# Attention's running states: summed by TensorE in PSUM and copied by ScalarE, in place of additions on VectorE

## The chip, the core and the metric

The kernel runs on one core of one Trainium2 chip, in one launch. A core has five engines with an instruction stream each: TensorE (PE in the profile; its weight loads are shown apart as PEld), VectorE (DVE), ScalarE (ACT), GpSimd (POOL) and SyncE (SP, which here only issues DMAs). They meet through semaphores. TensorE writes its results to PSUM, a memory in banks, from which VectorE and ScalarE read.

The metric is the device time of one execution, in microseconds, as the median of several runs.

## The reference

A group normalization and causal linear attention are added to x, then a group normalization and a chain of four Mamba blocks. The change touches the attention, whose core is this (x is 8 x 512 x 48 x 48, so 8 samples of L = 2304 positions with 8 heads of 64):

```python
def _feature(t):
    return jax.nn.elu(t) + 1.0
...
def step(S, qkv):
    q, k, v = qkv
    S = S + k[..., :, None] * v[..., None, :]
    o = jnp.einsum('nhk,nhkv->nhv', q, S)
    return (S, o)
_, outs = jax.lax.scan(step, S0, (Qs, Ks, Vs))
...
den = 1.0 / (jnp.einsum('nhld,nhld->nhl', Q, jnp.cumsum(K, axis=1)) + 1e-10)
num = _linear_causal_numerator(Q, K, V)
out = num * den[..., None]
...
x = x + _L0_conv_ref(_gn(x), L0_conv_Wq, L0_conv_bq, L0_conv_Wkv, L0_conv_bkv)
x = x + _L1_conv_ref(_gn(x), L1_conv_in_proj_w, ...)
```

For each head there is a running state S of 64 x 64, the sum of k v^T over all earlier positions. The kernel needs it only at the borders of blocks of 128 positions: within a block it uses the masked product of q and k.

## The kernel before

**The work.** Attention is cut into 8 samples x 4 pairs of heads x 6 chunks of 384 positions, 192 calls of the generator `chunk`. A chunk has NT = 3 blocks of T = 128 positions. Mamba is cut in the same way into 192 jobs (two streams of samples, taking turns); a job has 8 slots. A slot is four scans on VectorE (`scan`, L894, each over a decay that ScalarE writes to a PSUM bank, `decay`, L883), one product ahead of them (L873 on VectorE, L862 on GpSimd), one weighing by C on GpSimd (`weigh`, L906) and eight products on TensorE that gather the result (`gather`, L922). Before a job come its convolution (L698), gate (L709), SiLU, the small products for dt, B and C (L745, L758), and the softplus (L769).

**What sets the order.** The program writes out the order by hand. `slot` emits four scans, and between them calls `beside` twice, so that there are 16 half slots to a job. `chunk`, `prepare` and the other generators yield a due time in half slots and the number of PSUM banks they need next; `beside` steps those that are due and whose banks are free. So one chunk runs along with one job, always at the same place in it. Each engine executes its instructions in the order in which they were emitted.

**The banks.** Six PSUM banks (`spare`) are handed out to whoever takes one: chunks, job preparation and decays. ScalarE is up to three decays ahead of the scans (`DEPTH`, `ahead`); a bank that a scan or a chunk sets free is taken by a later decay.

**The state in a chunk.** `S` holds four states of 64 columns for both heads of the pair (128 partitions), one pair of heads over its six chunks. A chunk starts from the last state of the chunk before and makes the next three (`more`, two in the last chunk); `place` lists their columns, upward in even chunks and downward in odd ones, so that the last state of one chunk is the first of the next. Around the change:

- step `at(12)` takes a bank `both`. TensorE writes the denominators to its first six columns (L408) and the three sums k v^T of single blocks to columns 192 to 383 (`ds`, L413: for each block and each head one product of 64 x 64).
- step `at(14)`: VectorE reads the denominators (L416), takes the reciprocal (L417), and makes each state from the one before: a copy for the very first (L423), and otherwise an addition of `ds` to the state (L425). Each addition needs the last one's result. Then the bank is free.
- `at(15)`: ScalarE spreads the reciprocals over 64 columns (L429), TensorE turns them (L433), VectorE scales q (L438).
- `at(22)`: TensorE adds up x, S times q (L477) and v times the masked product (L486). The loop `while read[0] < m` at step `at(14)` holds the new states back until these products of the chunk before have been emitted.

All of these are float32. A float32 product appears as two TensorE records in the profile.

Of the kernel before, what the change touches and what calls it, by code (L numbers as in the profile page):

```python
# [17 lines left out]
P = 128  # L18
# [32 lines left out]
def attention_then_mamba_kernel(  # L51
# [12 lines left out]
    nc = tc.nc  # L64
# [17 lines left out]
    ident = cst[:, C_ID : C_ID + P]  # L82
# [200 lines left out]
    def chunk(m):  # L283


        b, o, c = parts[m]
        n = f"{b}_{o}_{c}"
        bank = Banks()
        NT = LC // T
        cols, tile_rows = slice(c * LC, (c + 1) * LC), slice(o * P, (o + 1) * P)  # L290
        subs = [slice(i * T, (i + 1) * T) for i in range(NT)]
        heads_of = [slice(par * 64, par * 64 + 64) for par in range(2)]

        def at(j, gap=1):
            return times[m] + j, gap

        def new(tag, bufs=1, shape=(P, LC)):
            return apool.tile(list(shape), F32, tag=tag, name=f"{tag}_{n}", bufs=bufs)
# [50 lines left out]
        S, stats, ksum = passes[b, o]  # L349
# [49 lines left out]
        kl, v = new("kl", 1, (P, NT, P)), new("v", 2, (P, NT, P))  # L399
# [8 lines left out]
            nc.tensor.matmul(den[:, 2 * i : 2 * i + 2], pr[:, subs[i]], hsel, start=True, stop=True)  # L408
        more = NT if c + 1 < NC else NT - 1
        ds = both[:, LC - NT * 64 : LC].rearrange("p (i d) -> p i d", i=NT)  # L410
        for i in range(more):
            for h in heads_of:
                nc.tensor.matmul(ds[h, i, :], kl[:, i, h], v[:, i, h], start=True, stop=True)  # L413
        yield at(14), 0
        rd = small.tile([P, 2 * NT], F32, tag="rd", name=f"rd_{n}", bufs=1)
        nc.vector.tensor_scalar_add(rd, den, 1e-10)  # L416
        nc.vector.reciprocal(rd, rd)  # L417
        while read[0] < m:
            yield "1w", 0
        place = range(NT + 1) if c % 2 == 0 else range(NT, -1, -1)  # L420
        for i in range(more):
            if c == 0 and i == 0:
                nc.vector.tensor_copy(S[:, place[1], :], ds[:, 0, :])  # L423
            else:
                nc.vector.tensor_add(S[:, place[i + 1], :], S[:, place[i], :], ds[:, i, :])  # L425
        bank.free()
        yield at(15), 0
        rdb = new("rdb", 1, (P, 2 * NT, 64))
# [15 lines left out]
        for sc in scs:  # L444
# [4 lines left out]
                start=True,  # L449
                stop=False,  # L450
                skip_group_check=True,
            )
        for i in range(NT):
            for h, sc in zip(heads_of, scs):
# [4 lines left out]
                    start=False,  # L459
                    stop=i == NT - 1,  # L460
                    skip_group_check=True,
# [11 lines left out]
        for i in range(NT):  # L473
            old = c > 0 or i > 0
            for h, sm in zip(heads_of, sms):
                if old:
# [4 lines left out]
                        start=False,  # L481
                        stop=False,
                        skip_group_check=True,
                    )
            for h, sm in zip(heads_of, sms):
# [4 lines left out]
                    start=False,  # L490
                    stop=i == NT - 1,
                    skip_group_check=True,
# [548 lines left out]
    def begin(latest):  # L1041

        nonlocal begun, put
        while counted and begins[counted[0]] - 4 <= half_no[0]:
            tasks.append(Task(statistics(counted.pop(0))))
        while put < len(parts) and times[put] - 6 <= half_no[0]:
            put += 1
            heads.append(Task(chunk(put - 1), before=heads[-1] if heads else None))
        while (
            begun < len(jobs)  # L1050
            and jobs[begun].start <= latest
            and jobs[begun].stream.block == jobs[begun].block
            and jobs[begun].stream.ready > jobs[begun].c
        ):
            tasks.append(Task(jobs[begun].prepare(), jobs[begun].start))
            begun += 1
# [241 lines left out]
```

## Time and profile before

| what | value |
|---|---|
| runs, median of 3 | 8507.66 us (8495.87 to 8511.29) |
| profiled execution, its own time | 8495.18 us |
| profiled execution, span from first to last instruction | 8493.4 us |
| TensorE's mean granted clock | 0.971 |
| scans on VectorE (L894) | 6144, busy 5448.0 us |
| state additions on VectorE (L425) | 512, busy 106.3 us |
| weighing on GpSimd (L906) | 1536, busy 4896.6 us |
| decays on ScalarE (L883) | 6144, busy 3422.1 us |
| gathering products on TensorE (L922) | 12288, busy 2374.3 us |

Busy times are of single engines and run beside each other, so they don't add up to the span. In lines of the profile `S<-S,bank` reads "writes S, reads S and a PSUM bank"; `L425` is a line of the kernel; `<-ACT bank L883` behind an idle time names what ended it, here a ScalarE instruction of line 883 that wrote a bank. Matmuls are pipelined: one record's length is its latency, and the distance between the starts of two records is what one costs in a row of them.

### The profile page before, as it was taken

The page shows a single profiled execution, that of the slowest core. Times are in us where ns is not written, and L with a number is a line of the kernel's source. Part 1 is how long each engine was busy: PE and PEld are TensorE (multiplying, and loading weights), DVE is VectorE, ACT ScalarE, POOL GpSimd, SP SyncE. Part 2 cuts the span into 40 slices and gives each one's busy share as a digit, 9 for nine tenths or more (in the row PEclk, how much of TensorE's full clock was granted, in tenths as well). Part 3 has the DMA queues.
Part 4 walks back from the last instruction along what each step waited for, and adds up shares of the span by engine and source line. Part 5 has one row for each costly group of instructions (what it writes and reads, how often), then busy time and mean ns, then how long its engine had stood idle before and what let it go on. Part 6 is the DMA issues. An engine that isn't in the chain of part 4 may idle for free. (4 is left out here: it accounts for less than half of the span.)

```text
span 8493.4 us, 124303 instructions
## 1 busy us (share of the span) xinstructions
PE 7728.9 (91%) x36482; PEld 3694.1 (43%) x36482; DVE 8077.7 (95%) x11078; ACT 6892.2 (81%) x14437; POOL 7761.5 (91%) x4235
## 2 busy tenths in 40 slices
PE   8799999999999999999999999999999999999965
PEld 4344444444444444444444444444444444444422
DVE  3799999999999999999999999999999999999998
ACT  3678888888888888888888888888888888888875
POOL 2689999999999999999999999999999999999998
PEclk9899999999999999999999999999999999999987
DMA  6567777767777777767777777777777777767655
GB/s 195 138 182 193 203 204 199 206 189 211 205 197 196 198 204 207 201 191 200 203 207 196 194 197 204 205 202 194 197 207 206 196 198 193 191 197 194 182 159 149
DMA packets 974426, 1654.38 MB, mean 195 GB/s; under 512 B 119337, under 2 KB 768169, under 8 KB 973618
## 3 DMA queue, kind: packets, MB, share of 16 engines
q1 hardware_dynamic: 973746, 1646.43, 70.6%
q8 instruction: 290, 4.75, 0.3%
q14 instruction: 390, 3.19, 0.1%
HBM read 1318.28 MB, written 327.68 MB: 194 GB/s over the span
## 5 line engine op out<-in xcount | busy, mean ns | idle before, releaser
L894 DVE TENSOR_TENSOR_SCAN u<-bank,u 128x385 f32<-128x385 f32 (+1 forms) x6144 | 5448.0, 937 | 138.5 <-ACT bank L883 136.6
L906 POOL TENSOR_TENSOR u<-u,C 128x1536 f32<-128x1536 f32 x1536 | 4896.6, 3188 | 498.3 <-DVE u L894 145.7
L883 ACT ACTIVATE bank<-dr,scales 128x385 f32<-128x385 f32 (+1 forms) x6144 | 3422.1, 578 | 788.1 <-DVE u L894 672.7
L922 PE MATMUL yp<-u,cst 128*64 128x384 f32 x12288 | 2374.3, 507 | 245.9 <-POOL u L906 126.8
L862 POOL TENSOR_TENSOR u<-B,dxr 128x512 f32<-128x512 f32 x1536 | 1973.4, 1285 | 47.7 <-DMA B<-scr 47.2
L873 DVE TENSOR_TENSOR u<-B,dxp 128x1024 f32<-128x1024 f32 x1536 | 1832.0, 1193 | 29.7 <-DMA B<-scr 24.2
L303 PE MATMUL bank<-xn,wq 128*128 128x384 f32 x4608 | 1741.1, 523 | 74.9 <-DVE u L894 39.6
L922 PEld LDWEIGHTS yp<-u,cst 128*64 128x64 f32 x12288 | 777.3, 138 | 1440.2 <-issue 926.3
L303 PEld LDWEIGHTS bank<-xn,wq 128*128 128x128 f32 x4608 | 869.1, 199 | 848.4 <-DVE u L894 139.9
L698 PE MATMUL bank<-xi,wk 128*128 128x384 f32 x3072 | 1107.4, 503 | 28.5 <-POOL xi L672 24.4
L698 PEld LDWEIGHTS bank<-xi,wk 128*128 128x128 f32 x3072 | 557.7, 191 | 575.9 <-issue 88.0
L315 ACT ACTIVATE ex<-bank,bqkv_sb 128x384 f32<-128x384 f32 x384 | 221.3, 576 | 470.7 <-PE bank L303 470.5
L883 ACT ACT_TABLE_LOAD x381 | 488.8, 1283 | 6.7
L811 POOL TENSOR_TENSOR dx<-delta,xs 128x384 f32<-128x384 f32 x384 | 387.3, 1009 | 33.0 <-ACT delta L769 33.0
L940 PE MATMUL bank<-yz,scales 128*128 128x384 f32 x768 | 305.0, 515 | 31.8 <-DVE yz L934 19.3
L433 PE MATMUL bank<-cst,rdb 128*128 128x128 f32 x576 | 102.9, 289 | 247.6 <-DVE u L894 244.1
L758 PE MATMUL bank<-dbc,steps_w 9*128 9x384 f32 x768 | 304.0, 515 | 3.1 <-ACT dbc L750 3.1
L709 PE MATMUL bank<-xi,scales 128*128 128x384 f32 x768 | 291.2, 493 | 10.6 <-ACT xs L734 8.8
L846 ACT COPY dxp<-dxr 128x512 f32<-128x512 f32 x384 | 226.7, 590 | 74.5 <-DMA dxr<-xscr 50.8
L745 PE MATMUL bank<-xs,scales 128*40 128x384 f32 x768 | 279.9, 486 | 0.3 <-ACT sm L467 0.3
L486 PE MATMUL bank<-sm,v 128*64 128x128 f32 x2304 | 253.4, 298 | 0.0
L734 ACT ACT_TABLE_LOAD x192 | 246.3, 1283 | 3.9 <-PE bank L698 0.6
(117 smaller groups left out, 7872.7 us busy)
## 6 DMA issues: line engine op xcount, KB each, us to landing
B<-scr SPq DMA_DIRECT2D x1536, 192.0 KB, 4.5
C<-scr SPq DMA_DIRECT2D x1536, 192.0 KB, 5.2
xn<-xn SPq DMA_DIRECT2D x192, 768.0 KB, 7.1
dr<-dscr SPq DMA_DIRECT2D x768, 192.0 KB, 3.8
dxr<-xscr SPq DMA_DIRECT2D x768, 192.0 KB, 4.9
dscr<-delta SPq DMA_DIRECT2D x192, 384.0 KB, 7.0
xscr<-dx SPq DMA_DIRECT2D x192, 384.0 KB, 2.4
xn<-in_x SPq DMA_DIRECT2D x48, 768.0 KB, 6.5
```

The source lines that it names most:

```text
L303: nc.tensor.matmul(ps, wqs[m // NC][:, kt, j * P : (j + 1) * P], xn[:, kt, :], start=(kt == 0), stop=(kt == 3),)
L698: nc.tensor.matmul(xc, wk[:, k, h * P : (h + 1) * P], xi[:, c0 + k : c0 + k + LC], start=(k == 0), stop=(k == 3),)
L709: nc.tensor.matmul(zp, w_gate[:, s, h * P : (h + 1) * P], xi[:, c0 + 3 : c0 + 3 + LC], start=True, stop=True,)
L758: nc.tensor.matmul(vp, steps_w[32:41, s, h * P : (h + 1) * P], dbc[32:41, :], start=True, stop=True)
L811: nc.gpsimd.tensor_tensor(dx[:, h, :], delta[:, h, :], xs[:, h, :], ALU.mult)
L862: nc.gpsimd.tensor_tensor(u[:, :, :, 1 + LC - TAIL :], self.B[s % 4][:, :, cols].unsqueeze(2).to_broadcast(shape), self.dxr[s // 4][:, :, ...
L873: nc.vector.tensor_mul(u[:, :, :, 1 : 1 + LC - TAIL], self.B[s % 4][:, :, cols].unsqueeze(2).to_broadcast(shape), self.dxp.unsqueeze(1).to ...
L883: nc.scalar.activation(dA[:, cols], self.dr[h][:, g, cols], AF.Exp, scale=w_a[:, self.w[1], 2 * h + g, q + j : q + j + 1],)
L894: nc.vector.tensor_tensor_scan(u[:, j, g, cols], dA[:, cols], u[:, j, g, cols], 0.0, ALU.mult, ALU.add,)
L906: nc.gpsimd.tensor_tensor(u[:, :, :, 0:LC], u[:, :, :, 1:], self.C[s % 4].unsqueeze(2).to_broadcast([P, NG, 2, LC]), ALU.mult,)
L922: nc.tensor.matmul(self.yp[g * 64 : g * 64 + 64, 0:LC], pair_sum, u[:, j, g, 0:LC], start=False, stop=(s % 4 == 3 and j == NG - 1), skip_g ...
L940: nc.tensor.matmul(self.xm[:, 0:LC], w_out[:, self.w[1], h, :], self.yz[:, h, :], start=(h == 0), stop=(h == 1),)
```

## The change

TensorE makes the running states itself, in the same columns of the same bank. An identity product first lays the old state `S[place[0]]` under all three new ones (from the second chunk on). Then the state after block i gets the products k v^T of all blocks 0 to i, added up in PSUM, in place of that of block i alone: twelve 64 x 64 products in place of six, or six in place of four in a last chunk. ScalarE copies all new states to `S` in one instruction, and the additions on VectorE go. `ds` is laid out in the order of the columns in `S`, so that the copy is one contiguous piece, also in odd chunks.

```diff
         more = NT if c + 1 < NC else NT - 1
         ds = both[:, LC - NT * 64 : LC].rearrange("p (i d) -> p i d", i=NT)
+        place = range(NT + 1) if c % 2 == 0 else range(NT, -1, -1)
+        low = min(place[1 : more + 1])
+        kept_states = slice(low, low + more)
+        if c:
+            nc.tensor.matmul(
+                ds[:, 0:more, :],
+                ident,
+                S[:, place[0], :].unsqueeze(1).to_broadcast([P, more, 64]),
+                start=True,
+                stop=False,
+                skip_group_check=True,
+            )
         for i in range(more):
-            for h in heads_of:
-                nc.tensor.matmul(ds[h, i, :], kl[:, i, h], v[:, i, h], start=True, stop=True)
+            for j in range(i + 1):
+                for h in heads_of:
+                    nc.tensor.matmul(
+                        ds[h, place[i + 1] - low, :],
+                        kl[:, j, h],
+                        v[:, j, h],
+                        start=c == 0 and j == 0,
+                        stop=j == i,
+                        skip_group_check=True,
+                    )
         yield at(14), 0
         rd = small.tile([P, 2 * NT], F32, tag="rd", name=f"rd_{n}", bufs=1)
         nc.vector.tensor_scalar_add(rd, den, 1e-10)
         nc.vector.reciprocal(rd, rd)
         while read[0] < m:
             yield "1w", 0
-        place = range(NT + 1) if c % 2 == 0 else range(NT, -1, -1)
-        for i in range(more):
-            if c == 0 and i == 0:
-                nc.vector.tensor_copy(S[:, place[1], :], ds[:, 0, :])
-            else:
-                nc.vector.tensor_add(S[:, place[i + 1], :], S[:, place[i], :], ds[:, i, :])
+        nc.scalar.copy(S[:, kept_states, :], ds[:, 0:more, :])
         bank.free()
         yield at(15), 0
```

## The prediction

> **What bounds the kernel now.** I read the page's busy shares, then the busy time by stretches, to see whether the start differs from the middle, then the groups of the lines that the change touches, then the timeline around one chunk of attention, and last the chain of waits through the same place.
>
> ```profile
> PE 7728.9 (91%) x36482; PEld 3694.1 (43%) x36482; DVE 8077.7 (95%) x11078; ACT 6892.2 (81%) x14437; POOL 7761.5 (91%) x4235
> ```
> ```profile
> 2000.00:3000.00 1000.00, 932.02 (x4462) 444.99 (x4462) 976.50 (x1328) 843.75 (x1778) 947.97 (x519) 0.99 0.73 199
> ...
> 0.00:340.00 340.00, 264.27 (x1325) 146.96 (x1327) 159.59 (x310) 151.06 (x305) 129.16 (x115) 0.92 0.59 176
> ```
>
> The second fence gives for two stretches their length and the busy us of PE, weight load, VectorE, ScalarE and GpSimd, then TensorE's clock, the DMA's share and GB/s. In the steady middle VectorE is busy 976 of 1000 us, the most of all; in the first 340 us it is busy 160 of 340, and nothing is gained there by relieving it.
>
> ```profile
> L425 DVE TENSOR_TENSOR S<-S,bank x512: 177/220/222, 46.5 to 8022.2; 128x64 f32<-128x64 f32 x171
> L423 DVE COPY S<-bank x32: 180/182/184, 46.3 to 7809.1; 128x64 f32<-128x64 f32 x32
> ...
>   ACT bank L883: 77.3, 143
> ```
>
> These are the state updates, 544 of some 0.2 us (shortest, median, longest in ns). ScalarE's next decay (L883) waited for the last of them 143 times, 0.54 us on average: it takes the PSUM bank that they set free.
>
> ```profile
> 7085.68 2.66 DVE L894 TENSOR_TENSOR_SCAN u<-bank,u 128x385 f32<-128x385 f32 x3 [0.79 <-ACT bank L883]
> ...
> 7086.64 0.57 PE L413 MATMUL bank<-v,kl 128*64 128x64 f32 x12
> ...
> 7087.04 1.46 PE L922 MATMUL yp<-u,cst 128*64 128x384 f32 x8
> ...
> 7088.26 0.14 DVE L416 TENSOR_SCALAR rd<-bank 128x6 f32<-128x6 f32 x1
> ...
> 7088.54 0.69 DVE L425 TENSOR_TENSOR S<-S,bank 128x64 f32<-128x64 f32 x3
> ...
> 7088.78 0.19 ACT L861 COPY u<-state 128x4 f32<-128x4 f32 x1
> 7089.15 1.80 DVE L894 TENSOR_TENSOR_SCAN u<-bank,u 128x385 f32<-128x385 f32 x2
> 7089.32 0.59 ACT L883 ACTIVATE bank<-dr,scales 128x385 f32<-128x385 f32 x1 [0.35 <-DVE S L425]
> ```
>
> One chunk in order of time. VectorE stands 0.79 us for ScalarE's first decay after a table load, then runs three scans, the denominator, its reciprocal and the three additions, and scans on. ScalarE stands 0.35 us for the additions.
>
> ```profile
> 7083.77 1.28 ACT L883
> ...
> 7085.68 0.51 DVE u L894
> ...
> 7088.75 0.23 DVE S L425
> ...
> 7089.15 0.95 DVE u L894
> ...
> 7090.13 0.59 ACT bank L883
> ...
> 7091.65 1.28 ACT L769
> ...
> 7093.83 4.56 PE bank L303 x8
> ```
>
> The chain of waits changes its engine several times in one round of some 42 us: ScalarE's table load and decay, VectorE's scans and additions, ScalarE again (decay, table load, softplus), then TensorE's projection. It can be followed from the end back to 6249 us, a quarter of the span, and its shares by engine are
>
> ```profile
> PE 8%; DVE 8%; ACT 6%; issue 2%; DMA 1%; POOL 1%; SPq 1%; POOLq 0%; DVEq 0%; ACTq 0%
> ```
>
> so no engine alone sets the pace. But of the 119 state additions in that part 90 stand on the chain, 0.76; I take 0.7 for the whole run, whose earlier part I can follow less well.
>
> [...] the mean granted clock is 0.971, and the eight L303 instructions take 4.56 us in the chain above but 2.85 us in most rounds (4015.18 us, for one).
>
> **The change part by part.** In the two programs the order of all other instructions is the same on every engine, DMA issues on SP and GpSimd's work included; only the state's instructions are exchanged in their places. No step is moved past a queue.
>
> VectorE loses 544 updates. What one chunk gains is the time from its first addition to the next instruction: 7088.54 to 7089.15, 0.61 us for three, and 0.353 us for the two of a last chunk (same difference there). Of the 192 chunks 11 lie in the first 410 us, where VectorE isn't short of time. The other 181 are 151 of three and 30 of two: 151 x 0.61 + 30 x 0.353 = 103 us.
>
> TensorE gets 1024 more 64x64 products (12 in place of 6, or 6 in place of 4), each shown as two records, and 160 identity products. From the timeline: twelve L413 records take 0.57 us, of which 0.22 is the length of the last, so a pair (two heads side by side) costs 0.07 us; six more pairs are 0.42 us. Eight L922 records of 384 columns take 1.46 - 0.49 = 0.97 us for three pair steps, 0.32 us or 0.84 ns a column; two records of 192 columns are another 0.32 us. Together 0.74 us for a chunk (0.42 for a first, some 0.36 for a last). It goes in between L413 and L922, where L922, the dt products (L758) and the next L922 follow; that next one stood 0.65 us for GpSimd, so the delay ends there. On the chain of waits L413 and L408 hardly appear, so I count 3% of 160 x 0.74 us, 4 us. Who could feel it is L416, which waits for the last of the group: it ended at 7087.21, L416 began at 7088.26, 1.05 us later, and this distance is 1.0 us or more in 178 of the 192 chunks, 11 of the 14 others being at the start. After the change 0.3 us is left. At the start the products are late already; 11 chunks at up to 0.5 us give 5 us.
>
> ScalarE gets 192 copies at 0.3 us, 56 us in all, at a place where it stood still. L861 ends at 7088.97; behind it come the copy (its wait, for L416's end at 7088.40, is over) and at about 7089.2 the decay, in place of 7089.32. What is queued behind the waiting copy is this decay, and VectorE's scans wait for that; it waited for the additions at the same place before. So ScalarE gains 0.1 us here, and at its next decay (7090.13, which waited for a scan that now ends 0.61 us earlier) about 0.43 us: by then it is busy with its own work. The path that goes on from here is ScalarE's, so what a chunk on the chain gains is nearer 0.45 us than 0.61 (0.3 for a last one): 151 x 0.45 + 30 x 0.3 = 77 us, 0.7 of it 54 us. Less 4 and 5 us: 45 us. The bank comes free some 0.2 us earlier as well, by the end of the copy against the end of the additions, for which I add 5 us. Of the profiled execution's 8495.2 us (span 8493.4) this leaves 8445 us. The median of the runs, 8507.7 us, is 12.5 us above that execution; 50 us off it is 8458 us.
>
> Bounds: the copy, 192 elements, between the 0.18 us of L917 with 4 elements and the 0.48 us of L400 with 384, so 0.3 us is safe to 0.15 us, 29 us in all if ScalarE has no slack. The identity product reads a repeated block and loads its weights behind a matrix of other shape; nothing in the trace has this, so its 0.32 us may be 0.6. [...] 60 of some 570 projections took over 4 us, 1.7 us too many each, up to 100 us in all, of which a shift may give or take 20.
>
> **The rivals.** First, hidden: VectorE only waits longer. It stands 136.6 us for decays already (158 times, 0.86 us), just ahead of the additions, and PE and ScalarE hold half of the chain; if the round's length is set by them, 0.61 us is given back at the next such wait. Against it: the additions come behind that wait, and the chain goes through them. It leaves 0 to 20 us gained, 8498 us. Second, the whole is gained: 103 us and earlier banks, 8400 us; against it, ScalarE's own work at 7090. Third, slower: L416 waits for the grown product group. It has 1.05 us of room, and the additions give 0.61 more, so this decides from a group that grows by over 1.66 us. It would, if a product that adds to the columns that the one before has just written can't overlap it: twelve new records at their full length of 0.22 us are 2.6 us. Halfway between this and 0.42 us, with the identity product's 0.32, the group grows by 1.9 us, and VectorE loses 0.24 us net in 181 chunks, 43 us: 8551 us. For it: L416 can wait so (50.5 us for L413, 11 times, at the start). Against it: L486 adds to one bank in the same way, and four of its records take 0.44 us at 4026.86 us.
>
> **How the numbers follow.** The forecast, 25 to 85 us gained, has 0.56; hidden 0.21; the whole 0.11; slower 0.12. The range goes from the whole gain (8400) to just above no change (8520), as the slower case lies mostly outside. 0.2% is 17 us, about what a measurement of this kernel can tell from no change: faster by more has the forecast, the whole and a third of hidden, 0.74; within it 0.14; slower 0.12.
>
> **What would show it.** Right: L416 rarely waits for the products; L883's wait for the additions is gone and a shorter one stands at the copy; VectorE's busy time falls by some 100 us and its idle time rises by about half of that; the copy takes 0.3 us. Wrong: a wait at L416 in most chunks, VectorE's waits for decays grown by 100 us, or projections at half clock in many more rounds.

## The result and the profile after

The changed kernel takes 8372.45 us (median of 4 runs, 8369.84 to 8376.44) against 8506.96 us before: a ratio of 0.9844, 95% interval 0.9827 to 0.9861, or 134.5 us less. That is more than the 103 us that VectorE's additions took in the part of the run where VectorE is short of time, and it lies below the forecast range of 8400 to 8520 us.

First the page's busy shares of the changed kernel, then its busy time by stretches, in the columns explained in the prediction.

```profile
PE 7760.3 (93%) x38850; PEld 3745.5 (45%) x38850; DVE 7971.6 (95%) x10534; ACT 6920.9 (83%) x14629; POOL 7757.7 (93%) x4235
```
```profile
2000.00:3000.00 1000.00, 952.77 (x4818) 460.13 (x4814) 978.13 (x1275) 865.77 (x1835) 964.35 (x527) 1.00 0.75 204
...
0.00:340.00 340.00, 266.09 (x1451) 150.01 (x1453) 147.57 (x266) 149.05 (x304) 124.46 (x113) 0.93 0.58 173
```

VectorE's busy time fell by 106 us (8077.7 to 7971.6), and its idle time by 18 us (from 415.7 to 397.6 us of the span) instead of growing: the round has become shorter by all of what it lost, and more. The other engines are busier per 1000 us, since their work is done in less time.

The same place in a round, from the timeline of the changed kernel (line numbers behind L426 have moved: L436 is the denominator, L437 its reciprocal, L909 the scans, L898 the decays, L937 the gathering products, L448 the turning of the reciprocals, L773 the dt products):

```profile
7105.80 0.52 PE L426 MATMUL bank<-v,kl 128*64 128x64 f32 x12
...
7106.15 1.46 PE L937 MATMUL yp<-u,cst 128*64 128x384 f32 x8
7106.58 0.14 DVE L436 TENSOR_SCALAR rd<-bank 128x6 f32<-128x6 f32 x1
7106.76 0.19 DVE L437 RECIPROCAL rd<-rd 128x6 f32<-128x6 f32 x1
7106.86 1.77 DVE L909 TENSOR_TENSOR_SCAN u<-bank,u 128x385 f32<-128x385 f32 x2
...
7107.20 0.31 ACT L440 COPY S<-bank 128x192 f32<-128x192 f32 x1
...
7107.54 1.09 ACT L898 ACTIVATE bank<-dr,scales 128x385 f32<-128x385 f32 x2
...
7111.52 2.85 PE L303 MATMUL bank<-xn,wq 128*128 128x384 f32 x8 [0.24 <-DVE u L909]
```

The scan follows the reciprocal at once. ScalarE's copy stands where its wait for the additions stood, and the decay comes behind it without idle time. The products end 0.27 us ahead of the denominator's read (median from the thirteenth chunk on), where it was 1.05 us: so the TensorE group has grown by 0.78 us, and the read hardly ever waits for it. The last line is the surprise: the eight projection records take 2.85 us here, where the round shown in the prediction had 4.56 us. TensorE's granted clock was 0.50 in that one, as the second window below shows. The trace's clock record knows two values, 1.00 (full) and 0.50 (half), in 192 stretches before and 92 after; all of them but the last of each trace are whole multiples of 3.41 us. What it says of those two rounds, in windows of this length, first before and then after (the first number behind the length is TensorE's busy time, the third from the end its granted clock):

```profile
7090.67:7094.09 3.42, 1.64 (x10) 0.71 (x7) 3.42 (x5) 3.37 (x7) 3.42 (x2) 1.00 0.93 236
7094.09:7097.50 3.41, 3.41 (x6) 1.72 (x6) 3.41 (x5) 2.81 (x6) 3.36 (x3) 0.50 1.01 245
```
```profile
7109.00:7112.41 3.41, 2.94 (x15) 1.43 (x15) 3.41 (x5) 3.36 (x6) 3.41 (x2) 1.00 0.98 237
7112.41:7115.83 3.42, 3.30 (x11) 1.48 (x9) 3.42 (x5) 3.41 (x9) 3.42 (x3) 1.00 0.89 265
```

Before, TensorE worked 1.64 us in one window, and the next one ran at half clock (0.50), with projections in it. After, it works 2.94 us at this place, and the next window has 1.00. Over the middle of the run (400 to 7900 us) the clock record has 63 stretches at half clock before, and 49 of them begin 5.4 to 7 us behind a chunk's denominator; after there are 14, one of them there. The idle time in question is TensorE's hole ahead of the turning of the reciprocals. In the timeline of the two rounds it is the number in brackets, before and after:

```profile
7093.07 0.52 PE L433 MATMUL bank<-cst,rdb 128*128 128x128 f32 x3 [1.54 <-DVE u L894]
```
```profile
7110.76 0.52 PE L448 MATMUL bank<-cst,rdb 128*128 128x128 f32 x3 [0.23 <-DVE u L909]
```

The table of waits has it for the whole run, before and after (total us, times, longest):

```profile
PE bank L433 <- DVE u L894: 244.1, 167, 1.6
```
```profile
PE bank L448 <- DVE u L909: 58.5, 165, 0.7
```

The change shortens this hole from both sides: the added products push the dt products ahead of it 0.78 us later, and VectorE, without the additions, ends it 0.6 us earlier. So there were two theories for the 134 us. Theory A: VectorE's removed time with what it pulls along. Theory B: besides that, a part is TensorE's clock.

### The profile page after: what moved, and what is told of

Read it like the earlier page. It is cut to its first block, busy times and chain, and to the rows that moved or that the text cites. A ratio compares the mean times of both kernels' runs of the same rounds, so it can differ in the third digit from the quotient of the medians.

```text
span 8369.2 us, 128536 instructions
## 1 busy us (share of the span) xinstructions
PE 7760.3 (93%) x38850; PEld 3745.5 (45%) x38850; DVE 7971.6 (95%) x10534; ACT 6920.9 (83%) x14629; POOL 7757.7 (93%) x4235
## 5 line engine op out<-in xcount | busy, mean ns | idle before, releaser
L909 DVE TENSOR_TENSOR_SCAN u<-bank,u 128x385 f32<-128x385 f32 (+1 forms) x6144 | 5441.5, 935 | 130.3 <-ACT bank L898 127.5
L898 ACT ACTIVATE bank<-dr,scales 128x385 f32<-128x385 f32 (+1 forms) x6144 | 3412.1, 578 | 684.2 <-DVE u L909 648.4
L937 PE MATMUL yp<-u,cst 128*64 128x384 f32 x12288 | 2375.2, 508 | 254.9 <-ACT yp L866 131.8
L303 PE MATMUL bank<-xn,wq 128*128 128x384 f32 x4608 | 1658.2, 502 | 101.2 <-POOL xn L327 48.1
L937 PEld LDWEIGHTS yp<-u,cst 128*64 128x64 f32 x12288 | 777.3, 138 | 1444.1 <-issue 1018.0
L303 PEld LDWEIGHTS bank<-xn,wq 128*128 128x128 f32 x4608 | 833.8, 191 | 839.0 <-DVE u L909 106.4
L315 ACT ACTIVATE ex<-bank,bqkv_sb 128x384 f32<-128x384 f32 x384 | 220.4, 574 | 408.5 <-PE bank L303 408.4
L773 PE MATMUL bank<-dbc,steps_w 9*128 9x384 f32 x768 | 304.8, 517 | 2.1 <-ACT dbc L765 2.1
```

Source lines behind the costliest of these rows:

```text
L303: nc.tensor.matmul(ps, wqs[m // NC][:, kt, j * P : (j + 1) * P], xn[:, kt, :], start=(kt == 0), stop=(kt == 3),)
L898: nc.scalar.activation(dA[:, cols], self.dr[h][:, g, cols], AF.Exp, scale=w_a[:, self.w[1], 2 * h + g, q + j : q + j + 1],)
L909: nc.vector.tensor_tensor_scan(u[:, j, g, cols], dA[:, cols], u[:, j, g, cols], 0.0, ALU.mult, ALU.add,)
L937: nc.tensor.matmul(self.yp[g * 64 : g * 64 + 64, 0:LC], pair_sum, u[:, j, g, 0:LC], start=False, stop=(s % 4 == 3 and j == NG - 1), skip_g ...
```

## The experiments

Each ratio is to the runs of the kernel before that were made in the same set (medians 8505.1, 8509.3 and 8510.4 us for the experiments whose names begin with e1, e2 and e3). The next two columns count the stretches at half clock in the middle of the run, in one trace of each kernel, and those of them that begin 5.4 to 7 us behind a denominator. The last is the hole, worked out from the records: the idle time ahead of the turning of the reciprocals, median from the thirteenth chunk on.

| kernel | median us | ratio to before, 95% interval | stretches | of these at the hole | hole, us |
|---|---|---|---|---|---|
| before | 8506.96 | | 63 | 49 | 1.53 |
| the change | 8372.45 | 0.9827 to 0.9861 | 14 | 1 | 0.23 |
| e1_dve_only | 8358.94 | 0.9809 to 0.9842 | 19 | 0 | 0.90 |
| e1_pe_only | 8453.86 | 0.9922 to 0.9952 | 13 | 1 | 0.88 |
| e1_warm_before | 8450.80 | 0.9919 to 0.9949 | 13 | 0 | 0.11 |
| e1_warm_after | 8397.87 | 0.9855 to 0.9884 | 14 | 2 | none |
| e2_work_elsewhere | 8572.92 | 1.0063 to 1.0093 | 50 | 40 | 1.54 |
| e2_dve_copy | 8407.67 | 0.9868 to 0.9897 | 15 | 0 | 0.49 |
| e2_act_twice | 8377.25 | 0.9834 to 0.9863 | 16 | 2 | 0.23 |
| e2_early_old | 8367.82 | 0.9820 to 0.9853 | 21 | 1 | 0.23 |
| e3_hole_3 | 8458.24 | 0.9922 to 0.9952 | 12 | 1 | 0.78 |
| e3_hole_1 | 8461.94 | 0.9925 to 0.9958 | 15 | 0 | 1.23 |

**VectorE's additions away, TensorE's work as before** (e1_dve_only), an edit of the changed kernel:

```diff
-        if c:
-            nc.tensor.matmul(
-                ds[:, 0:more, :],
...
-            for j in range(i + 1):
+            for j in (i,):
...
-                        start=c == 0 and j == 0,
+                        start=True,
```

> The states are not summed: TensorE makes the sums of single blocks alone, as in the kernel before, and ScalarE copies these to S (so S holds a block's own sum, and the later products read that). VectorE's additions are gone, TensorE's added work is not there. Theory A (the gain is VectorE's removed 0.61 us of a round, with what it pulls along): the same time as the changed kernel, 8372 us within 10. Theory B (a part of the gain comes from TensorE's clock, which stays up because the added products fill a hole in its work): 25 to 50 us of the gain go missing, 8397 to 8422 us, and the half-clock stretches that begin about 6 us behind the denominator's read are back in part (63 stretches in the middle of the run before, 14 after).

8358.94 us, 13.5 us faster than the changed kernel, and 19 stretches. Theory B's number failed: taking the products out did not bring the stretches back. The reason is the other side of the hole: VectorE ends it earlier, which leaves 0.90 us of 1.53, and this alone went with 19 stretches in place of 63. So this run holds both gains, and does not part them. By the medians the added products cost the change some 13 us, but the intervals of the two ratios overlap. The twelfth denominator begins at 332.4 us before, 332.9 here and 339.9 in the changed kernel, so 7 us of that lie in the start.

**TensorE's products alone** (e1_pe_only), an edit of the kernel before; the additions stay:

```diff
+        if c:
+            wide = 184 if more == NT else 128
+            nc.tensor.matmul(both[:, 6 : 6 + wide], ident, cst[:, 0:wide], start=True, stop=True)
         for i in range(more):
-            for h in heads_of:
-                nc.tensor.matmul(ds[h, i, :], kl[:, i, h], v[:, i, h], start=True, stop=True)
+            for j in range(i + 1):
+                for h in heads_of:
+                    to = ds[h, i, :] if j == i else both[h, LC : LC + 64]
+                    nc.tensor.matmul(to, kl[:, j, h], v[:, j, h], start=True, stop=True)
```

> The kernel before, with TensorE's added records at the same place and in the same number but written to columns of the bank that nobody reads; VectorE's additions stay. Theory A: no gain, 8507 us, or up to 10 us slower for the added work. Theory B: 20 to 50 us faster than before, 8457 to 8487 us, with most of the half-clock stretches gone.

8453.86 us: 51 us are gained, a little over the expected interval, by giving TensorE more to do, with nothing taken from anyone. Theory B holds, and theory A, which had no gain here, falls as the whole account. The projections show it in the table of groups: mean length of a record before, and here (ns, behind the busy us):

```profile
L303 PE MATMUL bank<-xn,wq 128*128 128x384 f32 x4608 | 1741.1, 523 | 74.9 <-DVE u L894 39.6 <-POOL xn L327 22.5 <-ACT delta L769 7.5
```
```profile
L303 PE MATMUL bank<-xn,wq 128*128 128x384 f32 x4608 | 1659.2, 503 | 81.1 <-DVE u L899 40.3 <-POOL xn L327 26.4 <-ACT delta L774 7.5
```

Nor did the added products make the rounds shorter in another way. From the twelfth denominator to the last, this trace is 46.6 us shorter than that of the kernel before. Taken round by round (from one denominator to the next, the same chunk in both), the 50 rounds that touch a stretch at half clock before and none here gain 52 us together, and the 113 at full clock in both gain nothing (2 us longer in all, median the same 41.96 us).

From here to the changed kernel, with the same work on TensorE and as few stretches, there are 81 us: that is what the additions' move to ScalarE gains by itself.

**Idle work at the hole, away from attention** (e1_warm_before, e1_warm_after; and with fewer products e3_hole_3, e3_hole_1):

```diff
                 vps.append(vp)
+            for _ in range(6):
+                nc.tensor.matmul(
+                    warm[:, LC : LC + P], ident, cst[:, 0:P], start=True, stop=True
+                )
             while spreading:
```

> The kernel before, with six idle 128 x 128 products (about 1.3 us) behind the dt products, written to columns that nobody reads, in every job; attention is untouched. Theory A: no gain, 8507 to 8525 us. Theory B: faster than before by 30 to 60 us, 8447 to 8477 us, with hardly a half-clock stretch in the middle left.

8450.80 us, 54 us faster, in the expected interval.

> The changed kernel with the same six idle products behind the dt products. Theory B: the hole is filled already and 14 stretches are left, so the time stays within 10 us of 8372 us, or falls by up to 15 us if the end of the run, where no attention runs, stays at full clock too. Theory A: same or up to 15 us slower.

8397.87 us, 25 us slower than the change, more than either theory had (the two intervals just overlap). The changed kernel had 14 stretches, and there are 14 here, so the 1.3 us of a round (an estimate: six products of two records with 128 columns, at the prediction's 0.84 ns a column) are only a load, and there is no hole left that would take it: the turning begins 5.41 us behind the denominator here and 4.18 us in the changed kernel (medians), and ScalarE waited 464.6 us for projections against 408.4 us.

> The kernel before with three idle 128 x 128 products (0.65 us) behind the dt products, just ahead of TensorE's hole: the same work as in the run with work elsewhere, at another place. Theory B: 8440 to 8475 us, with fewer than 20 half-clock stretches in the middle, against 8573 us and 50 there. If the place makes no difference to the clock, some 50 stretches and 8505 us or more.

> The same with one such product (0.22 us). [...] a part of the stretches goes, 8470 to 8500 us. [...] as with three; [...] as before, 8507 us.

8458.24 and 8461.94 us: one idle product of 0.22 us (by the same estimate) in a job has almost the whole effect of six, with 15 stretches against 13, and the 8470 to 8500 us did not come about. A round of e3_hole_1 at the same phase of the windows:

```profile
5141.38:5144.80 3.42, 1.94 (x12) 0.78 (x9) 3.42 (x5) 3.37 (x6) 3.42 (x2) 1.00 1.07 249
5144.80:5148.21 3.41, 3.41 (x12) 1.82 (x10) 3.41 (x5) 3.40 (x8) 3.37 (x3) 1.00 1.11 290
```

TensorE works 1.94 of 3.42 us here, 57%, and the next window has 1.00; before it was 1.64 us, 48%, and the next one had 0.50. The hole is 1.23 us in place of 1.53.

**The same idle work at another place** (e2_work_elsewhere), behind the running sum of k, in the kernel before:

```diff
+        for _ in range(3):
+            nc.tensor.matmul(kc_bank[:, LC : LC + P], ident, cst[:, 0:P], start=True, stop=True)
```

> The kernel before with three idle 128 x 128 products (0.65 us, about what the change adds) at another place of the round, behind the running sum of k, where TensorE has no hole. Theory B says that only the hole matters: the half-clock stretches stay (about 63 in the middle) and there is no gain, 8500 to 8570 us, slower as far as TensorE is on the path there. If any added work keeps the clock up, it gains like the run with the work beside the states, 8440 to 8475 us.

8572.92 us, 64 us slower, 3 us above the expected interval, with 40 stretches still at the hole. It is the same three products as in e3_hole_3, which gained 52 us. So TensorE's load as a whole did not decide it here: the same work left 50 stretches at this place and 12 at the hole. It also shows a price of added work at a busy place: 192 x 0.65 us (the estimate for three products) is 125 us, and half of that was lost. How much of it is TensorE's time isn't shown, since the reader of this bank waits for the three products too (ScalarE stands 28.3 us for it, 46 times).

**Who makes the copy** (e2_dve_copy, e2_act_twice), edits of the changed kernel:

```diff
-        nc.scalar.copy(S[:, kept_states, :], ds[:, 0:more, :])
+        nc.vector.tensor_copy(S[:, kept_states, :], ds[:, 0:more, :])
```
```diff
         nc.scalar.copy(S[:, kept_states, :], ds[:, 0:more, :])
+        nc.scalar.copy(S[:, kept_states, :], ds[:, 0:more, :])
```

> The changed kernel, but VectorE copies the new states, in one instruction of 192 elements, in place of ScalarE. If VectorE's time is what counts in a round (theory A), its 0.3 us come back in 181 rounds, 8 in 10 of it: about 45 us slower than the changed kernel, 8405 to 8430 us. If ScalarE is at its limit at this place, as the prediction had it, the copy taken from it makes up for that: 8372 to 8395 us.

> The changed kernel with ScalarE's copy made twice, one behind the other. Theory A (ScalarE has room here): within 10 us of the changed kernel, 8362 to 8385 us. If ScalarE is at its limit here, as the prediction had it, 0.3 us in most of 181 rounds is lost: 8400 to 8425 us.

On VectorE the copy costs 35 us (8407.67), in theory A's interval; its line in the table of groups:

```profile
L440 DVE COPY S<-bank 128x192 f32<-128x192 f32 x192 | 58.7, 306 | 0.0
```

So of 55 us in 181 rounds 0.63 is lost. A second copy on ScalarE costs 5 us (8377.25, 12 us between the twelfth and the last chunk in its trace), of 56 us that 181 copies of 0.31 us would be; the intervals overlap, so it is not shown to cost anything. ScalarE has room at this place, nearly all that is needed.

**The old way in the first 12 chunks** (e2_early_old):

```diff
+        early = m < 12
-        if c:
+        if c and not early:
...
-            for j in range(i + 1):
+            for j in (i,) if early else range(i + 1):
...
-        nc.scalar.copy(S[:, kept_states, :], ds[:, 0:more, :])
+        if not early:
+            nc.scalar.copy(S[:, kept_states, :], ds[:, 0:more, :])
+        for i in range(more if early else 0):
...
```

> The first 12 chunks update the states on VectorE as before, the others as in the changed kernel. TensorE's added products cost 7 us up to the twelfth chunk (332 us in the run with VectorE's additions alone left out, 340 us in the changed kernel), and this gives them back: 8360 to 8370 us, faster than the changed kernel by 3 to 12 us. If the loss at the start is made up later anyway, the same time.

8367.82 us. The twelfth denominator begins at 331.7 us in place of 339.9, so the start's loss is real, but of these 8 us only 5 are seen in the median, and the intervals of the two ratios overlap: it is the fastest kernel with the full computation here, not shown to be faster than the change.

## Why the prediction was wrong

**TensorE's clock was the missing term.** The bound said that a shift "may give or take 20". It counted the 60 slow projections and their price, and then treated them as chance. They weren't chance: 49 of 63 stretches began at one place of the round, behind the 1.54 us that TensorE stood ahead of the turning of the reciprocals, and both halves of the change shorten that hole. The term of +-20 us measured -51 us when the hole was filled from one side alone (e1_pe_only), and it can be had from either side, once.

**What a round gains was too small.** The sum let a round on the chain gain 0.45 us, not 0.61, because ScalarE would be "busy with its own work" at its second decay; with 0.7 of the rounds on the chain that made 54 us. That is 0.30 us for each of 181 rounds. At equal work on TensorE the move gained 81 us (e1_pe_only to the change), which is 0.79 of VectorE's 103 us. Between the two traces, 160 rounds from the twelfth chunk on are at full clock in both. Their gain is 0.64 us in the median (0.39 us in a last chunk, with two additions) and 0.53 us in the mean, 85 us together, and nine in ten of them gain 0.2 us or more. So most rounds gain all of the 0.61 us, and nearly all rounds gain something: both the 0.45 us and the 0.7 were too low. A second copy on ScalarE, which should have cost 0.3 us a round if ScalarE were at its limit, cost 5 us in all. The two terms, 81 and 51 us, make 132 of the 134.5 us, as they must, since e1_pe_only lies between the two kernels; that each stands for one cause is what the rounds show. The count of the first chunks was off too, without weight: 13 denominators, not 11, are read in the first 410 us, some 1 us of the sum.

**What held.** The copy was put at 0.3 us, and the profile has 0.31. The product group was to grow by 0.74 us and leave 0.3 us ahead of the denominator; it grew by 0.78 and leaves 0.27. The start was to lose 5 us and lost 7. The rival "L416 waits" did not come about: VectorE's table of waits has the same 11 waits at the start as before.

```profile
DVE rd L436 <- PE bank L426: 56.4, 11, 13.3
```

The rival "hidden" fell too: VectorE's wait for decays is 127.5 us (147 times), not longer than the 136.6 us before. "The whole is gained" was the nearest, and its 103 us come close to what the move gained, but its sum of some 107 us had nothing for the clock, and the earlier banks that it added were not tested alone. The mean clock of 0.971 and projections of 4.56 us in place of 2.85 said that the clock fell, and not where in a round. What was missing was to set the clock record beside the round.

What stays open: how much of the 13.5 us between e1_dve_only and the change is real. The two traces differ by 10.2 us: 7 us lie in the start, 2.4 us between the twelfth and the last chunk (7554.1 against 7556.5), the rest behind it.

## What to carry to other kernels

Look at where in a round the clock falls, not only at its mean: here the stretches at half clock began at one place, a little more work there, or an earlier end of the wait, was worth more than it cost, and the same work at a busy place was a loss. When a change moves a wait of TensorE, ask for both sides of the idle time around it. And before a saving is cut down because another engine may be at its limit, double that engine's work at the place and see.

## What was not expected of the hardware

TensorE did some work in every window that half clock followed in the middle of the run (11 to 81% of it, before and after). Before, one of 3.41 us in which it was busy 48% of the time was followed by one at half clock (7090.67 us; of the 63 windows ahead of a stretch the middle half all show 48%, worked out from the records). In e3_hole_1, one at this place with 57% (5141.38 us) was followed by full clock. Counted from the clock record and the TensorE records in the middle of the run: before, 53 of the 61 windows at full clock in which TensorE was busy for less than half of the time were followed by half clock, and 10 of the 2065 others; with the change, 12 of 17 and 2 of 2157. What sets the clock isn't shown by these counts: there are exceptions on both sides, and the ends of the busy time are modelled. A round, 41.96 us in the median, is 12.3 windows and no whole number of them, so the windows fall differently in each: before, 93 of the 176 rounds had a window at full clock that ended 5.4 to 7 us behind the denominator, and 49 of these were followed by half clock. One product of 0.22 us in a round decided 48 us of a run of 8500 us.
